# A two-layer graph attention kernel: full-width transpositions, one key product per half of the nodes, second-layer sums kept in PSUM

## The chip, the cores and the metric

One core of a Trainium2 chip runs the whole program. The metric is the device time of one execution in microseconds (us); a kernel's time is the median over its runs. The engines are named PE or TensorE (matrix products; PEld is its loading of weights), DVE or VectorE, ACT or ScalarE, POOL or GpSimd, and SP or SyncE, which only issues DMAs.

## What is computed

Eight graphs of 2048 nodes with 64 features share one 0/1 adjacency matrix (`adj`, 2048 x 2048 int32, denser for low node numbers). Two attention layers without learned scores are followed by two normalisations:

```python
def _gat_layer(h, mask, b):
    scores = jnp.einsum('...nd,...md->...nm', h, h)
    scores = jnp.where(mask, scores, -1e16)
    attn = jax.nn.softmax(scores, axis=-1)
    return jnp.einsum('...nm,...md->...nd', attn, h) + b

mask = graph + jnp.eye(N) > 0
h = jnp.einsum('bnc,hdc->bhnd', x, Wh)                  # 4 heads
cat = transpose(_gat_layer(h, mask, bh)).reshape(B, N, H * D)
z = leaky_relu(cat, 0.2)
h2 = jnp.einsum('bnk,dk->bnd', z, Wo)
z2 = leaky_relu(_gat_layer(h2, mask, bo), 0.2)
out = layernorm(z2) * gamma + beta
return layernorm(x + out)
```

## The kernel before

`gat_kernel` runs `fast_kernel` and then tests a flag; only where the flag is set does `general_kernel` run as well. In all runs told of here the flag stays 0. Everything below is `fast_kernel`, whose instructions stand in a hand-written order; each engine works through its own in that order.

The first 56 nodes ("hubs") attend to all nodes. The other 1992 are cut into 166 sets of 12 (nodes s, s + 166, ...), and a set attends only to the union of its members' neighbours, at most 128 nodes. So a set needs: a list of 128 node numbers (`index`), a gather of those nodes' rows for all eight graphs (`gather`, L727, an indirect DMA on POOL), the rows turned so that features lie on partitions (`turn`, L509), scores (L760 in the first layer, L923 in the second), a mask subtracted on DVE (L763, L928), an exp on ACT (L767, L931), and the weighted sum (values; L778, L943). A column of ones beside the features gives the softmax's denominator. All products are fp32; each of them appears in the trace as two matmul instructions.

The stages:

- *Hub stage*, `for i in range(NB)`, 16 blocks of 128 nodes. Per block: load x (L464, ACT's queue), save it as rows of `table1` in DRAM (L467, SP's queue), turn it (L509, tile `px`), two hub scores (L579), mask (L583), exp (L586), two hub values (L597). Beside this the adjacency is loaded in 48 pieces (`load_adj`, L647), turned into bf16 0/1 on POOL (L649), and summed with powers of two over a set's 12 members (`make_keys`, L669, on PE, in two rounds of 84 and 82 sets) into keys that hold a member mask and the node's number. `pick` then takes the 128 largest keys with max and match-replace on DVE (L684, L686); its jobs are spread over the loop by `some` and the hub stage's own loop. At most six blocks run before the first round is loaded, and three loads of the second round are issued per block from i = 8 on.
- `hub_end`, once per half of the graphs: the hubs' second-layer rows.
- *First-layer loop*, 83 groups of two sets, software-pipelined over i = -3 .. 85: gathers for group i + 5, scores i + 1, turn i + 3, `turn_values` (L789), `columns` (L743, the queries), values i + 1, `project` (L524, the head weights), `second_maps` (L800), `second_rows` (L805). PSUM has two tags with two buffers each, "s" (turn, scores) and "o" (oty, o, cat). `keep_rows` (L809) writes second-layer rows to `table2` in DRAM.
- *Second-layer hub*, w = -2 .. 8, on blocks of `table2`.
- *Second-layer units*, 42 units of four sets: `scores2`, `turn_group`, `values2`, whose sums are copied to SBUF (L947), written to DRAM (`back`, L950) and read back in blocks of ten sets (120 partitions) by `norm`, with 17 such norms as lists of jobs spread over later units. `norm` computes on DVE, with a square on ACT (L992) and a power on POOL (L998).
- The tail: the last norms, stores (L1035), the flag.

Of the kernel before, what the change touches and what calls it, by code (L numbers as in the profile page):

```python
# [27 lines left out]
F32 = mybir.dt.float32  # L29
# [328 lines left out]
def fast_kernel(ctx: ExitStack, tc: tile.TileContext, x, adj, Wh, bh, Wo, bo, gamma, beta, out, flag):  # L358
# [10 lines left out]
    ROW = B * K1  # L369
    NS = (N - HUB) // SET  # L370
    NG = NS // 2
    ROUNDS = ((0, 84), (84, NS - 84))
    M = SET * H
    HN = HUB // 2
    SEG, KEEP = 8, 32
    SW = N // SEG
    assert NS * SET == N - HUB and NG * 2 == NS

    const = ctx.enter_context(tc.tile_pool(name="const", bufs=1))
    rowp = ctx.enter_context(tc.tile_pool(name="rowp", bufs=12))  # L380
    work = ctx.enter_context(tc.tile_pool(name="work", bufs=2))
    small = ctx.enter_context(tc.tile_pool(name="small", bufs=4))
    psum = ctx.enter_context(tc.tile_pool(name="psum", bufs=2, space=bass.MemoryType.PSUM))
    dram = ctx.enter_context(tc.tile_pool(name="scratch", bufs=1, space=bass.MemoryType.DRAM))
    early_ctx = ExitStack()
    early = early_ctx.enter_context(tc.tile_pool(name="early", bufs=1))

    def two(name, tag="s"):

        return psum.tile([P, 2, 512], F32, tag=tag, name=name)  # L390
# [4 lines left out]
    def rows_tile(name):  # L395
        return rowp.tile([P, B, K1], F32, tag="rows", name=name)
# [6 lines left out]
    offdiag = const.tile([P, P], BF16, name="offdiag")  # L403
    nc.vector.tensor_scalar(offdiag, ident, -1.0, 1.0, OP.mult, OP.add)
    ones = const.tile([P, 1], F32, name="ones")
    nc.gpsimd.memset(ones, 1.0)
    shifts = const.tile([P, 3], F32, name="shifts")
    nc.gpsimd.memset(shifts[:, 0:1], -SHIFT1)
    nc.gpsimd.memset(shifts[:, 1:2], -SHIFT2)
    nc.gpsimd.memset(shifts[:, 2:3], EPS)  # L410
    mhalf = const.tile([P, B], F32, name="mhalf")
    nc.gpsimd.memset(mhalf, -0.5)
    bits = const.tile([P, SET], I32, name="bits")
    for k in range(SET):
        nc.vector.memset(bits[:, k:k + 1], N << k)
    powers = early.tile([84, SET, 84], BF16, name="powers")
    for k in range(SET):
        nc.vector.tensor_scalar(powers[:, k, :], ident[:84, :84], float(1 << k), None, OP.mult)
    number = early.tile([84, SEG, SW], U16, name="number")
    nc.gpsimd.iota(number, [[1, SEG], [SEG, SW]], base=0, channel_multiplier=0)  # L420

    wnat = early.tile([P, H, C], F32, name="wnat")
    whT = const.tile([P, H * D], F32, name="whT")
    gram = const.tile([P, H, P], F32, name="gram")
    wos = early.tile([D, H * D], F32, name="wos")
    woT = const.tile([P, HP, D], F32, name="woT")
    bhp = const.tile([P, HP], F32, name="bhp")
    bob = const.tile([P, D], F32, name="bob")
# [5 lines left out]
    back = dram.tile([NS, SET, ROW], F32, name="back")  # L434
    backh = dram.tile([HUB, 2, Q * K1], F32, name="backh")

    rall = const.tile([P, NG + 2, 8], F32, name="rall")
    NL = (NS + 9) // 10
    rall2 = const.tile([P, NL + 1, 8], F32, name="rall2")
    nc.gpsimd.memset(rall[:, NG:, :], 1.0)  # L440
    nc.gpsimd.memset(rall2, 1.0)
    over = const.tile([P, 2, SEG + 1], F32, name="over")
    nc.gpsimd.memset(over, 0.0)

    xT = const.tile([P, Q, N], F32, name="xT")
    own = const.tile([P, NG * 96 + 16], F32, name="own")
    nc.gpsimd.memset(own, 0.0)
    ownh = const.tile([P, 2, 2 * 2 * HN], F32, name="ownh")
# [4 lines left out]
    es = [const.tile([P, 912], F32, name=f"e{k}") for k in range(2)]  # L453
    rowts = [const.tile([P, 2, K1], F32, name=f"rowt{k}") for k in range(4)]
    for t in rowts:
        nc.gpsimd.memset(t, 1.0)
# [4 lines left out]
    def load_x(i):  # L461
        t = xrow[i] = rows_tile(f"x{i}")
        nc.vector.memset(t[:, :, D:K1], 1.0)
        nc.scalar.dma_start(out=t[:, :, :D], in_=x[:, i * P:(i + 1) * P, :].rearrange("b p c -> p b c"))  # L464

    def save_x(i):
        nc.sync.dma_start(out=table1[i * P:(i + 1) * P, :], in_=xrow[i].rearrange("p b k -> p (b k)"))  # L467

    hubraw = [early.tile([HUB, 2, 512], I32, tag="raw", name=f"hubraw{k}", bufs=3) for k in range(2)]
    load_x(0)  # L470
    for k in range(2):
        nc.sync.dma_start(out=hubraw[k], in_=adj[0:HUB, k * 1024:(k + 1) * 1024].rearrange("n (a m) -> n a m", a=2))
# [6 lines left out]
    nc.gpsimd.dma_start(out=bob, in_=bo.partition_broadcast(P))  # L479
    nc.gpsimd.dma_start(out=gam, in_=gamma.partition_broadcast(P))  # L480
    nc.gpsimd.dma_start(out=bet, in_=beta.partition_broadcast(P))
    load_x(2)
# [10 lines left out]
    nc.gpsimd.memset(gram, 0.0)  # L493
# [18 lines left out]
    def invert(op, r, osb, parts, k):  # L512

        v = op[:parts, :, :k * K1].rearrange("p s (q c) -> p s q c", q=k)
        nc.vector.reciprocal(r, v[:, :, :, D])
# [694 lines left out]
```

## Time and profile before

| | us |
|---|---|
| median of 3 runs (1602.45 to 1607.83) | 1607.18 |
| the profiled execution | 1601.0 |
| its span, first to last instruction | 1599.1 |
| PE busy | 1165.8 (73%), 35983 matmul instructions |
| DVE, ACT, POOL busy | 694.8, 439.3, 454.7 |
[...]

Durations of the sections below come from this one execution. Matmuls overlap: one row's duration is that from its start to its modelled end, so the pace of a group of matmuls is read from the start of a group to the start of the next. "issue" as a releaser means that the engine stood idle and the profile shows nothing that it waited for.

### The profile page before, as it was taken

Reading aid. Unit: us, or ns where it says so; the run is one execution under the profiler, and the core shown is the slowest. Engines: PE = TensorE matmul, PEld = TensorE weight load, DVE = VectorE, ACT = ScalarE, POOL = GpSimd, SP = SyncE. Lnnn points to the kernel's source line nnn. Section 1 sums busy time; section 2 is a strip of 40 time slices with the busy share of each in tenths; the row PEclk is TensorE's granted clock in tenths of the full one; section 3 lists DMA queues with packets and bytes.
Section 4 is the critical chain, followed back from the end, with each engine's and each line's share of the span. In section 5 each row is a group of like instructions: output and inputs, shape, how many; then the busy total and the mean of one; then the engine's idle time right before and its main releaser. Section 6 shows DMA issues by size and latency. Waiting matters only on the chain.

```text
span 1599.1 us, 76844 instructions
## 1 busy us (share of the span) xinstructions
PE 1165.8 (73%) x35983; PEld 1032.3 (65%) x35983; DVE 694.8 (43%) x1342; ACT 439.3 (27%) x735; POOL 454.7 (28%) x468
## 2 busy tenths in 40 slices
PE   5887643878788888888888876777777877777720
PEld 4565432777677777777777765676767766777620
DVE  5392210566554444444444441232444444445465
ACT  1111210333333333333433442221212212222210
POOL 6411113122222222222222200133434444343411
PEclk9756865999899999999999986777666677666755
DMA  7622113122222222222222203234454444444420
GB/s 168 180 78 72 68 62 99 46 76 77 62 79 82 73 76 81 77 72 75 78 77 75 77 13 129 69 97 119 109 139 110 109 119 135 114 118 115 126 65 18
DMA packets 98838, 144.45 MB, mean 90 GB/s; under 512 B 44608, under 2 KB 60944, under 8 KB 98512
## 3 DMA queue, kind: packets, MB, share of 16 engines
q0 software_dynamic: 26688, 88.51, 20.2%
q1 hardware_dynamic: 55184, 46.75, 10.3%
q10 hardware_dynamic: 16640, 4.20, 1.4%
q8 instruction: 284, 4.65, 1.2%
q14 instruction: 42, 0.34, 0.1%
HBM read 122.44 MB, written 16.97 MB: 87 GB/s over the span
## 4 chain that ended last, share of the span: by engine, by line
PE 53%; DMA 13%; issue 13%; DVE 11%; ACT 4%; POOL 2%; SPq 1%; another core or an unknown queue 1%; ACTq 0%; POOLq 0%; DVEq 0%
PE t L509 13%; DMA raw<-in_adj_dram 13%; PE s L923 12%; PE oty L743 6%; PE s L760 5%; DVE y L749 4%; PE o L943 3%; PE cat L524 3%; ACT otb L793 2%; PE oty L789 2%; PE cat L805 2%; PE cat L800 2%; POOL a L649 1%; DVE e L763 1%
## 5 line engine op out<-in xcount | busy, mean ns | idle before, releaser
L727 POOL DMA_INDIRECT g<-table,index x332 | 321.2, 967 | 872.0 <-PE o L778 464.1
L923 PE MATMUL s<-own,xTg 64*64 64x12 f32 x5312 | 197.6, 242 | 104.3 <-issue 102.9
L509 PE MATMUL t<-ident,g 64*64 64x64 f32 x10624 | 260.1, 262 | 16.0 <-issue 15.8
L923 PEld LDWEIGHTS s<-own,xTg 64*64 64x64 f32 x5312 | 171.0, 191 | 133.1 <-issue 127.3
L509 PEld LDWEIGHTS t<-ident,g 64*64 64x64 f32 x10624 | 243.1, 175 | 20.9 <-issue 20.2
L760 PE MATMUL s<-y,xTg 64*64 64x48 f32 x5312 | 121.7, 220 | 31.3 <-issue 31.1
L760 PEld LDWEIGHTS s<-y,xTg 64*64 64x64 f32 x5312 | 107.8, 134 | 41.7 <-issue 41.1
L743 PE MATMUL oty<-xT,gram 128*64 128x96 f32 x1280 | 125.0, 345 | 6.7 <-issue 6.7
L809 DVE COPY rowt<-cat 128x128 f32<-128x128 f32 x83 | 24.3, 293 | 213.4 <-ACT own L903 213.0
L749 DVE COPY y<-oty 128x384 f32<-128x384 f32 x80 | 68.8, 860 | 108.4 <-PE oty L743 108.4
L767 ACT ACTIVATE e<-e,shifts 128x768 f32<-128x768 f32 x83 | 77.7, 936 | 123.2 <-DVE e L763 123.2
L778 PEld LDWEIGHTS o<-g,e 128*64 128x64 f32 x2656 | 98.8, 144 | 11.5 <-ACT e L767 7.7
L778 PE MATMUL o<-g,e 128*64 128x65 f32 x2656 | 100.1, 228 | 7.4 <-ACT e L767 5.5
L743 PEld LDWEIGHTS oty<-xT,gram 128*64 128x64 f32 x1280 | 92.3, 149 | 17.2 <-issue 10.4
L649 POOL TENSOR_SCALAR a<-raw 84x1024 bf16<-84x1024 int32 (+1 forms) x48 | 49.8, 1037 | 183.2 <-DMA raw<-in_adj_dram 170.3
L531 ACT ACTIVATE z<-cat,bhp 128x192 f32<-128x192 f32 x166 | 60.8, 418 | 113.1 <-PE cat L524 109.8
L793 ACT COPY otb<-oty 128x384 f32<-128x384 f32 x83 | 39.7, 479 | 168.1 <-DVE y L749 152.5
L890 ACT COPY xTg<-t 128x1024 f32<-128x1024 f32 x83 | 84.5, 1018 | 4.6 <-PE t L509 4.6
L597 PEld LDWEIGHTS oh<-x,e 128*112 128x112 f32 x512 | 71.2, 229 | 19.8 <-ACT e L586 12.8
L597 PE MATMUL oh<-x,e 128*112 128x65 f32 x512 | 76.0, 317 | 10.6 <-ACT e L586 10.6
L998 POOL TENSOR_TENSOR st<-st,mhalf 120x8 f32<-120x8 f32 (+2 forms) x36 | 62.2, 1728 | 71.7 <-DVE st L997 42.4
L996 DVE TENSOR_REDUCE st<-sq 120x8 f32<-120x512 f32 (+2 forms) x36 | 24.7, 685 | 131.9 <-ACT sq L992 96.2
(151 smaller groups left out, 1544.4 us busy)
## 6 DMA issues: line engine op xcount, KB each, us to landing
raw<-in_adj_dram SPq DMA_DIRECT2D x24, 336.0 KB
raw<-in_adj_dram SPq DMA_DIRECT2D x24, 328.0 KB
g<-table,index POOLq DMA_INDIRECT x332
table<-x SPq DMA_DIRECT2D x16, 260.0 KB
gh<-table SPq DMA_DIRECT2D x16, 260.0 KB
x<-in_x_dram ACTq DMA_DIRECT2D x16, 256.0 KB
table<-rowt SPq DMA_DIRECT2D x166, 24.4 KB
back<-o2sb SPq DMA_DIRECT2D x164, 24.4 KB
```

What stands on the lines that cost most here:

```text
L509: nc.tensor.matmul(v[half(p), r, j, q, :], rows[half(r), 2 * q + p, :D], ident[half(r), half(r)], start=True, stop=True)
L597: nc.tensor.matmul(hubo[t][:HW // 2, s, b * K1:(b + 1) * K1], e[:, c0:c0 + HW // 2], xrow[i][:, 4 * t + b, :], start=(i == 0 and b == 0), ...
L649: nc.gpsimd.tensor_scalar(a[:n], raw[:n], 1.0, 0.0, OP.min, OP.max)
L727: nc.gpsimd.indirect_dma_start(out=t.rearrange("p b k -> p (b k)"), out_offset=None, in_=table, in_offset=bass.IndirectOffsetOnAxis(ap=ind ...
L743: nc.tensor.matmul(py[half(p), h // 2, 192 + h % 2 * 96:192 + (h % 2 + 1) * 96], gram[:, h, half(p)], src, start=True, stop=True)
L749: nc.vector.tensor_copy(y.rearrange("p n (a b) -> p a b n", a=2), py[:, :, 192:384].rearrange("p a (b n) -> p a b n", b=2))
L760: nc.tensor.matmul(sp[half(r), p, (q * 2 + j) * M:(q * 2 + j + 1) * M], xt[half(p), r, j, q, :], y[half(p), (j * Q + q) * M:(j * Q + q + 1 ...
L767: nc.scalar.activation(e[:, :16 * M], e[:, :16 * M], AF.Exp, bias=shifts[:, 0:1], scale=1.0)
L778: nc.tensor.matmul(op[half(p), j, q * K1:(q + 1) * K1], e[:, c0:c0 + 64], rw[:, 2 * q + p, :], start=True, stop=True)
L793: nc.scalar.copy(ot.rearrange("c h (p n) -> c h p n", p=2), pt[:, :, :Q * M].rearrange("c p (n h) -> c h p n", h=H))
L890: nc.scalar.copy(t, tp)
L923: nc.tensor.matmul(sp[half(r), p, c0:c0 + SET], xt[half(p), r, s % 2, q, :], own[half(p), (s * Q + q) * SET:(s * Q + q + 1) * SET], start= ...
```

## The change

`turn` uses `nc.tensor.transpose` with a 128 x 128 identity: rows of two graphs lie side by side (`[P, Q, PW]`, PW = 130, a one at both ends), and one instruction turns both. `columns` uses the whole block-diagonal `gram`, on contiguous copies made on POOL (`own_rows`). The adjacency is loaded with members and sets together on 120 partitions, so one product over all members gives a key. `second_rows` and `turn_values` also become transposes. The first-layer loop gets a new order and four PSUM tags with one buffer each (S, T, C, O); `keep_columns` moves from DVE to ACT, the copy to `own` from ACT to DVE, and `keep_values` becomes two copies. Nine of 34 adjacency pieces and the second `pick` move into this loop. In the second layer row tiles have 20 buffers, all turned rows are copied on ACT, `values2` sums two units into one PSUM tile (the second adds to the columns that zeros in its weights leave alone), and `norm` reads them there; x for it is loaded from `x`, and `bo` is added in `keep_rows`. There are 21 norms of two units, and one for the hubs. The core of the diff:

```diff
-    def turn(tp, j, rows):
-        v = tp.rearrange("c r (j q i) -> c r j q i", j=2, q=Q)
+    def turn(tp, rows):
         for q in range(Q):
-            for p in range(2):
-                for r in range(2):
-                    nc.tensor.matmul(v[half(p), r, j, q, :], rows[half(r), 2 * q + p, :D], ident[half(r), half(r)],
-                                     start=True, stop=True)
+            nc.tensor.transpose(tp[:, q * P:(q + 1) * P], rows[:, q, 1:1 + P], ident)
...
     def hub_values(i, t):
+        for v in range(2):
             for k in range(2):
                 for p in range(2):
-                    nc.tensor.matmul(hubo[t][:HW // 2, s, b * K1:(b + 1) * K1], e[:, c0:c0 + HW // 2],
-                                     xrow[i][:, 4 * t + b, :], ...)
+                    for u in range(2):
+                        nc.tensor.matmul(hubo[t][half(u), v, ...], es[t][:, c0:c0 + 64],
+                                         xrow[i][:, 2 * t + k, sums(p)], ...)
...
     def load_adj(r, t, m):
-        raw = early.tile([84, 2, 512], I32, tag="raw", name=f"raw{r}_{c}_{t}", bufs=3)
-        nc.sync.dma_start(out=raw[:n], in_=byset[s0:s0 + n, 2 * t:2 * t + 2, c * 512:(c + 1) * 512])
+        raw = early.tile([120, NCH], I32, tag="raw", name=f"raw{r}_{t}_{m}", bufs=3)
+        nc.sync.dma_start(out=raw[:np_], in_=byset[:, s0:s0 + ns, m * NCH:(m + 1) * NCH])
...
+    def own_rows(g):
+        t = held["x", g] = work.tile([P, GM], F32, tag="xo", name=f"xo{g}", bufs=3)
+        src = xT[:, :, HUB:].rearrange("c q (k s) -> c s q k", s=NS)[:, 2 * g:2 * g + 2]
+        nc.gpsimd.tensor_copy(t.rearrange("c (s q k) -> c s q k", s=2, q=Q), src)
...
     for i in range(-3, NG + 3):
...
+        sp = one(f"s{i}", "S")
+        if 0 <= i - 3 < NG:
+            second_rows(i - 3, sp[:GM, 1, 384:512])
+        if 0 <= i - 2 < NG:
+            second_maps(i - 2, sp[:, 0, 384:384 + GM])
         if 0 <= i + 1 < NG:
+            scores(i + 1, sp)
+            weigh(i + 1, sp)
+        if 0 <= i < NG:
+            turn_values(i, op)
+            keep_values(i, op)
+        if 0 <= i + 3 < NG:
+            tp = one(f"t{i + 3}", "T")
+            for j in range(2):
+                turn(tp[:, j, :], rows[1, 2 * (i + 3) + j])
+        if i < NG:
+            cat = one(f"cat{i}", "C")
+        if 0 <= i + 3 < NG:
+            columns(i + 3, cat)
+        if 0 <= i < NG:
+            project(held.pop(("ot", i)), cat, GM)
+        if 0 <= i + 1 < NG:
+            op = one(f"o{i + 1}", "O")
+            values(i + 1, op)
...    # then DVE: own, keep_rows, leak, some(2), invert, some(3); ACT: xTg, leaky, keep_columns
     def values2(op, sets, e, a, more):
         for k, s in enumerate(sets):
             rw = rows.pop((2, s))
             for f in range(2):
                 for t in range(4):
+                    q, p = 2 * f + t % 2, t // 2
+                    nc.tensor.matmul(op[t * 32:(t + 1) * 32, f, k * W2 + p:k * W2 + p + K1], e[:, p * Q + q, k, :],
+                                     rw[:, q, sums(p)], start=(a == 0 and k == 0), stop=(k >= more), ...)
-        nc.scalar.copy(o[:, :nb], op[:, :nb, :4 * K1])
-        for t in range(4):
-            nc.sync.dma_start(out=dst, in_=...)          # to back
...
+    for u in range(-1, NU + 6):
+        if u + 4 < NU:
+            for s in sets[u + 4]:
+                gather(table2, s, 2, rows2)
+        a = (u + 1) % 2
+        if u + 1 < NU:
+            scores2(bank2(f"s2_{u + 1}", "S"), sets[u + 1], es2[a], a)
+        if u + 3 < NU:
+            turn2(u + 3)
+        if u + 1 < NU:
+            if a == 0:
+                op = bank2(f"o2_{u + 1}", "O")
+            values2(op, sets[u + 1], es2[a], a, len(sets[u + 2]) if a == 0 else 0)
+            if a == 1:
+                spread(u, norm_sets((u + 1) // 2, op))
+        work_on(u)
```

## Rows read from the trace of the kernel before

**Rows 1.** Busy time by stage: PE, PEld, DVE, ACT, POOL (instructions), clock, DMA share, GB/s.

```profile
0.00:80.00 80.00, 57.39 (x631) 42.45 (x631) 38.95 (x84) 14.34 (x18) 42.20 (x61) 0.87 0.71 174
80.00:258.00 178.00, 108.59 (x1104) 83.43 (x1103) 62.97 (x151) 28.49 (x33) 30.20 (x40) 0.65 0.20 67
258.00:284.00 26.00, 11.70 (x113) 8.77 (x115) 4.03 (x10) 3.14 (x8) 10.42 (x11) 0.50 0.45 126
284.00:959.00 675.00, 552.41 (x19587) 502.24 (x19584) 319.57 (x643) 264.96 (x498) 145.68 (x154) 0.98 0.26 71
959.00:1019.00 60.00, 37.61 (x1295) 33.57 (x1298) 10.43 (x20) 15.82 (x16) 9.40 (x10) 0.73 0.36 113
1019.00:1532.00 513.00, 397.69 (x13280) 361.76 (x13275) 223.69 (x366) 108.35 (x155) 204.74 (x186) 0.69 0.42 113
1532.00:1599.00 67.00, 0.36 (x10) 0.09 (x2) 35.20 (x72) 4.19 (x8) 12.07 (x7) 0.50 0.16 40
```

**Rows 2.** Longest waits between 80 and 258 us: us in total, times, longest.

```profile
POOL a L649 <- DMA raw<-in_adj_dram: 144.3, 22, 17.0
```

**Rows 3.** PE in order of time, hub blocks: start us, us, count.

```profile
220.32 0.99 PE L579 MATMUL sh<-yh,xT 64*64 64x224 f32 x16
221.24 1.79 PE L597 MATMUL oh<-x,e 128*112 128x65 f32 x16
...
51.02 3.25 PE L597 MATMUL oh<-x,e 128*112 128x65 f32 x16
```

**Rows 4.** PE in order of time, one first-layer group; idle time and releaser in brackets.

```profile
738.92 1.52 PE L743 MATMUL oty<-xT,gram 128*64 128x96 f32 x16
740.26 1.12 PE L778 MATMUL o<-g,e 128*64 128x65 f32 x32
741.98 0.44 PE L805 MATMUL cat<-ident,own 128*64 128x128 f32 x4 [0.61 <-ACT otb L793]
...
744.04 0.87 PE L760 MATMUL s<-y,xTg 64*64 64x48 f32 x43 [0.41 <-issue]
...
744.77 1.13 PE L509 MATMUL t<-ident,g 64*64 64x64 f32 x62
```

**Rows 5.** PE in the last first-layer groups, and the window table around them.

```profile
945.57 1.10 PE L760 MATMUL s<-y,xTg 64*64 64x48 f32 x64
946.49 0.65 PE L789 MATMUL oty<-ident,osb 48*64 48x48 f32 x32
949.00 1.25 PE L778 MATMUL o<-g,e 128*64 128x65 f32 x32 [1.87 <-ACT e L767]
...
933.50:949.50 16.00, 11.68 (x516) 10.96 (x510) 7.53 (x14) 7.52 (x16) 0.00 (x0) 1.00 0.05 13
```

**Rows 6.** Groups by line and form: busy us, mean ns, idle before and releasers.

```profile
L793 ACT COPY otb<-oty 128x384 f32<-128x384 f32 x83 | 39.7, 479 | 168.1 <-DVE y L749 152.5 <-DVE rall L515 15.7
...
L684 DVE MAX8 cand<-keys 82x8 f32<-82x256 f32 x32 | 13.1, 417 | 0.3
...
L700 PE MATMUL pb<-ident,best 84*128 84x84 f32 x1 | 0.4, 372 | 2.2 <-DVE best L684 2.2
```

**Rows 7.** Second-layer units: a turn on PE, two window rows, the groups' line for scores2.

```profile
1300.27 3.71 PE L509 MATMUL t<-ident,g 64*64 64x64 f32 x125
...
1305.60:1310.60 5.00, 2.96 (x57) 2.40 (x57) 0.16 (x1) 1.12 (x2) 3.14 (x4) 0.77 0.57 160
1311.00:1316.00 5.00, 5.00 (x208) 4.93 (x211) 2.00 (x5) 0.62 (x2) 1.67 (x1) 0.59 0.34 85
...
L923 PE MATMUL s<-own,xTg 64*64 64x12 f32 x5312 | 197.6, 242 | 104.3 <-issue 102.9 <-DVE xTg L1148 0.4
```

**Rows 8.** PE in order of time, in hub_end.

```profile
272.54 1.02 PE L618 MATMUL hh<-zh,woT 128*64 128x112 f32 x8 [8.40 <-issue]
```

**Rows 9.** The tail: DVE and SP's queue in order of time.

```profile
1538.93 0.20 DVE L973 RECIPROCAL rall<-y 120x8 f32<-120x8 f32 x1 [5.97 <-DMA y<-back]
...
1560.74 29.80 SPq L1035 DMA_DIRECT2D out_dram<-y  x24
```

More of the change, by code (lines that the diff above doesn't have):

```diff
@@ L723, in fast_kernel, with gather @@
     held = {}
-    def gather(table, s, layer):
-        t = rows[layer, s] = rows_tile(f"g{layer}_{s}")
-        nc.gpsimd.indirect_dma_start(out=t.rearrange("p b k -> p (b k)"), out_offset=None, in_=table,
+    def gather(table, s, layer, new):
+        t = rows[layer, s] = new(f"g{layer}_{s}")
+        nc.gpsimd.indirect_dma_start(out=t.rearrange("n q c -> n (q c)"), out_offset=None, in_=table,
                                      in_offset=bass.IndirectOffsetOnAxis(ap=index[:, s:s + 1], axis=0))
-    def turn_group(layer, g, tag):
-        tp = two(f"t{layer}_{g}", tag)
-        for j in range(2):
-            turn(tp, j, rows[layer, 2 * g + j])
-        t = work.tile([P, 2, 512], F32, tag="xTg", name=f"xTg{layer}_{g}", bufs=3)
-        held["T", layer, g] = t
-        return tp, t
@@ L818, in fast_kernel, with some @@
     hub_columns()
+    picks = []
+    def some(n):
+        for _ in range(n):
+            if picks:
+                picks.pop(0)()
+    for e in es:
+        nc.vector.memset(e[:, 4 * HW:], 1.0)
     pend = None
-    pieces = list(load_adj_jobs)
-    picks = []
     for i in range(NB):
@@ L874, in fast_kernel @@
         if 0 <= i - 1 < NG:
             leak(held["z", i - 1])
+        if 0 <= i + 3 < NG:
+            t = held["T", 1, i + 3] = work.tile([P, 2, 512], F32, tag="xTg", name=f"xTg{i + 3}", bufs=3)
+            nc.scalar.copy(t, tp)
+        if 0 <= i < NG:
+            held["z", i] = leaky(cat, GM, f"z{i}")
+        if 0 <= i + 3 < NG:
+            keep_columns(i + 3, cat)
         if i >= 0:
             some(2)
[L878 to L881 removed]
@@ L882, in fast_kernel @@
-        if 0 <= i < NG:
-            turn_values(i, oty)
-        if 0 <= i + 3 < NG:
-            columns(i + 3, oty)
-            keep_columns(i + 3, oty)
-        if 0 <= i < NG:
-            keep_values(i, oty)
-        if 0 <= i + 3 < NG:
-            nc.scalar.copy(t, tp)
         if 0 <= i + 1 < NG:
-            values(i + 1)
+            invert(i + 1, op)
         if i >= 0:
-            cat = two(f"cat{i}", "o")
-        if 0 <= i - 2 < NG:
-            second_rows(i - 2, cat[:, 1, 256:384])
@@ L897, in fast_kernel @@
-        if 0 <= i - 1 < NG:
-            second_maps(i - 1, cat[:, 0, 256:384])
-        if 0 <= i < NG:
-            project(held.pop(("ot", i)), cat, 96)
-            held["z", i] = leaky(cat, i, 96)
-        if 0 <= i - 1 < NG:
-            nc.scalar.copy(own[:, (i - 1) * 96:i * 96], cat[:, 0, 256:352])
-        if 0 <= i - 2 < NG:
-            keep_rows(i - 2, cat[:, 1, 256:384])
-        if i >= 0:
-            some(1)
-    assert not picks
-    early_ctx.close()
-    late = ctx.enter_context(tc.tile_pool(name="late", bufs=2))
@@ L915, in scores2 @@
-    def scores2(sp, sets, e):
-        n = len(sets) * SET
+            more(2)
+            some(3)
+            done = all(t // 3 > k3 for r, t, m in pieces)
+            if k3 < nk and done:
+                make_keys(1, k3, late_two)
+                k3 += 1
+                if k3 == nk:
+                    picks = pick(1)
+    assert not picks and not pieces and k3 == nk
+    begin.close()
+    stage.close()
+    late = ctx.enter_context(tc.tile_pool(name="late", bufs=2))
+    psum2 = ctx.enter_context(tc.tile_pool(name="psum2", bufs=1, space=bass.MemoryType.PSUM))
@@ L1110, in fast_kernel @@
             hub_turn(w + 1)
+        elif w + 1 < NB // 2 + 2 and w + 1 >= NB // 2:
+            turn2(w + 1 - NB // 2)
         if 0 <= w - 1 < NB // 2:
             hub_values2(w - 1)
-    o = late.tile([P, 2, 4 * K1], F32, tag="o2", name="o2h")
-    nc.scalar.copy(o[:, 0], oh2[:, 0, :Q * K1])
-    for p in range(2):
-        nc.sync.dma_start(out=backh[:, p, :], in_=o[p * 64:p * 64 + HUB, 0, :])
-    NU = (NS + 3) // 4
-    sets = [list(range(4 * u, min(4 * u + 4, NS))) for u in range(NU)]
-    jobs = {}
```

740 lines of the change are left out of this document (394 added, 346 removed).

## The prediction

> **What bounds the kernel now.** I read the stage table first [rows 1], because an average over the program hides five different limits. Its rows show the hub stage up to 258 us, hub_end, the first-layer loop (675 us for 83 groups, 8.1 us each with filling and draining), the second-layer hub (60 us), the second-layer units (513 us for 42, 12.2 us each) and a tail of 67 us. They add up to the span of 1599.1 us; the profiled execution reports 1601.0 us, and the median of the runs is 1607.18 us, so I put 2 us and then 6 us on top of a sum of stages.
>
> In the hub stage the adjacency loads set the pace after 80 us. Traffic falls from 174 to 67 GB/s there while the DMA engines are only 20% busy [rows 1], and the conversions of the 24 loads with 82 partitions wait 144.3 us for data [rows 2]. A load that keeps few engines busy is slow; it is not that bandwidth is used up. PE itself needs, where nothing holds it, 0.99 us for hub scores and 1.79 us for hub values, and 3.25 us for the values when its clock is at half [rows 3].
>
> In the first-layer loop PE is the bound: its groups follow each other [rows 4], with 0.61 us of waiting for ScalarE and some tenths in which the profile names no releaser. The clock is 0.98 [rows 1].
>
> In the second-layer units PE runs at a mixed clock of 0.69 [rows 1] and is also starved of instructions. In 5.0 us beside four gathers on GpSimd it starts 57 matmuls, in 5.0 us without them 208 [rows 7]; the matmuls of scores2 alone stand 102.9 us behind "issue" [rows 7]. The same hits others: in hub_end PE loses 8.40 us this way [rows 8], while GpSimd issues gathers (11 instructions in that stage [rows 1]). In the tail VectorE waits 5.97 us for rows written to DRAM and read back, and the last 24 stores are queued on SP for 29.80 us [rows 9].
>
> **The change, part by part.**
>
> *Hub stage.* The loads become 120 partitions of 4 KB (12 members by 10 sets, half a row). No row shows this shape. If it runs as the first 24 loads did, at 174 GB/s [rows 1], 25 loads of 0.49 MB, 4.2 MB of x and 4.3 MB of saved rows are 20.8 MB, or 120 us, below what the engines need. Per block i, PE does two hub scores, two hub values (now 16 half-width products instead of 8) and one transposition. Half-width values take 1.12 us for 32 instructions [rows 4], so a block takes 2 x (0.99 + 1.12) + 4 x 0.14 = 4.8 us at full clock, and 1.8 times that, 8.7 us, at half (3.25 / 1.79 [rows 3]). I take 7.7 us: the clock is 0.65 there [rows 1], and for some seven blocks VectorE has six pick jobs each beside its other work (some 0.9 us a job: 0.42 [rows 6], about the same again for replacing and a little for loading). Sixteen blocks are 123 us (80 to 160). With 26 us of hub_end [rows 1], which the early gathers starve as before, and about 25 us of beginning, the loop starts at 175 us instead of 284 (150 to 210): **-109 us**. The memsets and selections that move on GpSimd's queue stand ahead of its conversions, a few us that the hub mask on VectorE hides; without that cover they delay the first block by as much.
>
> *The price of a transposition.* Each is now one instruction of 128 columns over the whole array, in place of four products of 64 columns that are two instructions each. Nearest rows: the values, 35 ns for 65 columns on half the array (1.12 us / 32 [rows 4]), thus 70 ns for both halves and 138 ns for 128 columns. Below it stands one old turn instruction, 18 ns (1.13 us / 62 [rows 4]); above it the kernel's only true transpose, 372 ns, alone and not pipelined [rows 6]. I take 0.14 us at full and 0.28 us at half clock.
> [...]
>
> *First-layer loop.* Removed per group: 56 of 64 turn instructions, 28 of 32 in turn_values, 3 of 4 in second_rows, 8 of 16 in columns, whose strided read moves to GpSimd as own_rows. Twelve transpositions are 1.7 us against 1.13 + 0.65 us [rows 4, 5], a draw; columns falls from 1.34 us (738.92 to 740.26) to about 0.7. But order and PSUM change too: one buffer per tag, and project now stands ahead of values, behind keep_values, which waits on ScalarE behind the exp. So I count the chain, not PE. The last groups, which have neither turn nor columns, show it bare: scores from 945.57, values at 949.00 after 1.87 us of waiting [rows 5]; less 1.0 us of scores this is 2.4 us for subtracting and exp. Added: keep_values, now two copies, 0.7 us (between one of 0.48 us [rows 6] and two of them). Then project 0.4, values 1.12, second_maps 0.45, second_rows 0.1 and scores 1.0 us. The sum is 2.4 + 0.7 + 0.4 + 1.1 + 0.5 + 1.0 = 6.1 us. PE's 1.7 + 0.7 us of other work lie in the 3.1 us before project, so they cost nothing; at half clock they would be 4.8 us and stick out. Two gathers a group still starve scores (0.4 us here: 744.04 stands 0.41 us late [rows 4]), so 6.6 us (6.1 to 7.6). keep_columns moves to ScalarE, behind leaky: whose turn it delays is the next exp, 2 us away. own and keep_rows on VectorE stand behind weigh, ahead of invert; GpSimd's own_rows stands behind two gathers that had idled. Bias rows (bob) in keep_rows cost nothing there.
> 83 x 6.6 = 548 us. The second pick runs inside the loop: 58 jobs at five a group are 4.5 us on VectorE beside some 3.2 (319.57 us [rows 1] less some 50 of picks, over 83), so about twelve groups take 7.9 us, +16. Filling and draining, one group longer, 21. Together 585 us for 675: **-90 us** (-130 to 0).
>
> *Second-layer hub.* Scores of both blocks now go before either subtraction, but exp, the copy of xTg and scores still follow each other. 57 us for 60: **-3** (-12 to +5).
>
> *Second-layer units.* Scores2 (128 instructions) and values2 (64) stay; 128 turn instructions, 3.8 us at 30 ns [rows 7], become 16 transpositions, 2.2 to 4.5 us. All 320 take 7.7 us at the rate of the better window; the other 4.5 of 12.2 us are starvation and hand-overs. GpSimd's gathers, with 20 row buffers, no longer wait for values2, but stand behind the power operations of the norms in GpSimd's queue, which come once a unit; so the burst drifts toward scores2 again. I take 11.0 us (9 to 12.4): -0.3 for turn, -0.9 for 96 matmuls that can no longer be starved. VectorE loses the copy of xTg and gains nothing. Values2 of a pair's first unit waits for the previous pair's first norm step; 1.5 us, under scores2. SP's per-pair 16 issues replace about as many. 42 x 11.0 + 3 = 465 us: **-48 us** (-135 to +8).
>
> *Tail.* Sums are read from PSUM, so the trip to DRAM goes, and one pair's norm with the rest of three others remains: some 20 us of VectorE, 5 us of hand-overs, 10 us for eight stores (29.80 / 24 each [rows 9]), 1 us for the flag. 36 us for 67: **-31 us** (-40 to -15).
>
> **Sum.** 175 + 585 + 57 + 465 + 36 = 1318 us of span, 1320 us as the profiled execution tells it, and 1325 us beside the median.
>
> **The rivals.**
> *(A) The units gain nothing*: half clock makes 16 transpositions 4.5 us and the burst meets scores2 in full, 12.4 us a unit, +59: 1384 us. For it: the 0.69 clock; against: fewer instructions to starve.
> *(B) The first-layer loop falls to half clock.* [...] Against: in the last groups the clock stayed at 1.00 for 16 us with 1.87 us of waiting a group [rows 5]. Then the chain's PE part, 3.0 us, becomes 5.4 and the period 8.5: 83 x 1.9 = +158, 1483 us.
> [...]
> *(C) The new load shape is as slow as the old second round*: hub stage unchanged, nine more loads in the loop, +110: 1435 us.
> *(D) Starvation goes with the instructions*: 8.7 us a unit, -97: 1228 us.
> *(E) Slower.* Single buffers put everything on one chain. If PE runs at half clock and each of its two bursts costs the chain 1.1 us (two gathers are half of the 5.0 us in which 151 of 208 starts are lost [rows 7]), a group takes 8.5 + 2.2 = 10.7 us, +340: 1665 us. It decides from 10.0 us a group ((675 + 191 - 37) / 83), where it has eaten the 191 us gained elsewhere. Against it: starvation hides in PE's waiting.
>
> **How the numbers follow.** Forecast 0.45, A 0.22, D 0.15, B 0.08, C 0.05, E 0.05. The range, 1225 to 1455 us, takes in the forecast's own bounds (1240 to 1420), A, C and most of D; B, E and the rest of D are left out, under two in ten. A measurement of this kernel can tell about 0.3%. Only E is slower: faster 0.94, same 0.01, slower 0.05.
>
> **What would show it.** Hub: the loop's first turn near 175 us and DMA above 100 GB/s before it. Loop: 6 to 7 us between values, PE waiting for ScalarE ahead of project, clock near 1. Units: 16 instead of 128 turn matmuls each, gaps in scores2 beside gathers. Tail: no wait for DRAM. I am wrong if the loop's clock falls, if project waits for more than exp and keep_values, or if a transposition costs over 0.2 us at full clock.

## The result and the profile after

The changed kernel takes 1391.67 us (median of four runs, 1388.97 to 1392.80) beside 1605.24 us for the kernel before in the same runs: a ratio of 0.867, 95% interval 0.8645 to 0.8689. That is 214 us faster, within the range of 1225 to 1455 us, and 67 us above the forecast of 1325. Its profiled execution has a span of 1390.4 us.

The stages of the changed kernel, in the columns of [rows 1]: from, to, length, then PE, PEld, DVE, ACT and POOL busy (instructions), clock, DMA share, GB/s. In order: hub stage, hub_end, first-layer loop, second-layer hub, units, tail.

```profile
0.00:152.00 152.00, 102.95 (x1717) 72.05 (x1717) 83.69 (x184) 42.85 (x51) 59.74 (x136) 0.94 0.60 157
152.00:166.40 14.40, 6.32 (x58) 3.90 (x58) 4.28 (x13) 2.64 (x6) 0.00 (x0) 0.65 0.02 5
166.40:829.00 662.60, 541.88 (x11724) 465.03 (x11724) 287.93 (x735) 291.47 (x581) 192.91 (x257) 0.98 0.29 78
829.00:887.00 58.00, 38.57 (x876) 32.43 (x876) 11.39 (x21) 19.38 (x20) 18.78 (x22) 0.80 0.53 166
887.00:1360.00 473.00, 358.48 (x8600) 321.52 (x8596) 205.59 (x389) 127.76 (x163) 219.56 (x187) 0.71 0.38 101
1360.00:1390.40 30.40, 0.19 (x2) 0.11 (x2) 18.93 (x41) 1.89 (x3) 8.52 (x5) 0.50 0.13 28
```

Against the terms of the sum:

| stage | before | forecast | after | forecast missed by |
|---|---|---|---|---|
| start of the loop | 284 | 175 | 166.4 | -8.6 |
| first-layer loop | 675 | 585 | 662.6 | **+77.6** |
| second-layer hub | 60 | 57 | 58 | +1 |
| units | 513 | 465 | 473 | +8 |
| tail | 67 | 36 | 30.4 | -5.6 |

One term is wrong, and by more than the whole miss: the loop got 12 us shorter where 90 were forecast. So the question is what holds a group at 7.74 us (the distance from one exp to the next in the steady part) when its chain was counted at 6.1.

Here is one group of it, PE and then POOL in order of time (start us, us, line, operands, count; in brackets the idle time before and its releaser):

```profile
571.11 0.84 PE L792 MATMUL s<-y,xTg 64*64 64x48 f32 x32
572.35 0.34 PE L792 MATMUL s<-y,xTg 64*64 64x48 f32 x6 [0.41 <-issue]
573.11 0.66 PE L792 MATMUL s<-y,xTg 64*64 64x48 f32 x26 [0.41 <-issue]
573.70 0.60 PE L831 MATMUL o<-ident,osb 112*128 112x112 f32 x4
574.14 1.04 PE L510 MATMUL t<-ident,g 128*128 128x128 f32 x8
575.01 1.03 PE L778 MATMUL cat<-xo,gram 128*128 128x96 f32 x8
576.55 0.56 PE L529 MATMUL cat<-otb,whT 64*64 64x96 f32 x16 [0.51 <-ACT otb L839]
577.04 1.15 PE L814 MATMUL o<-g,e 128*64 128x65 f32 x32
...
570.27 0.97 POOL L765 DMA_INDIRECT g<-table,index  x1 [1.49 <-PE o L814]
571.55 0.95 POOL L765 DMA_INDIRECT g<-table,index  x1 [0.30 <-issue]
```

And one of the last groups, for which nothing is left to gather:

```profile
800.39 1.15 PE L792 MATMUL s<-y,xTg 64*64 64x48 f32 x64
801.47 0.60 PE L831 MATMUL o<-ident,osb 112*128 112x112 f32 x4
801.90 1.04 PE L510 MATMUL t<-ident,g 128*128 128x128 f32 x8
802.78 1.03 PE L778 MATMUL cat<-xo,gram 128*128 128x96 f32 x8
804.34 0.56 PE L529 MATMUL cat<-otb,whT 64*64 64x96 f32 x16 [0.53 <-ACT otb L839]
804.83 1.15 PE L814 MATMUL o<-g,e 128*64 128x65 f32 x32
```

Without gathers the 64 matmuls of scores go from 800.39 to 801.47, 1.08 us; with them from 571.11 to 573.70, 2.59 us, with two gaps that stand behind "issue". Everything else in the two groups is alike, even the 0.5 us that PE waits for ScalarE ahead of project, and the groups without gathers follow each other in 6.25 us. The 1.5 us of difference is the whole gap between 6.25 and 7.74, and it falls at the same place in each group, because the gathers are released by the last product of values ("PE o L814") and scores comes soon after.

### The profile page after: what moved, and what is told of

Its sections match the earlier page's. It is cut to its first block, busy times and chain, and to the rows that moved or that the text cites. A ratio compares the mean times of both kernels' runs of the same rounds, so it can differ in the third digit from the quotient of the medians.

```text
span 1390.4 us, 50953 instructions
## 1 busy us (share of the span) xinstructions
PE 1048.4 (75%) x22965; PEld 895.0 (64%) x22965; DVE 611.8 (44%) x1380; ACT 486.0 (35%) x823; POOL 499.5 (36%) x606
## 4 chain that ended last, share of the span: by engine, by line
PE 52%; issue 21%; DVE 14%; ACT 7%; POOL 3%; DMA 2%; ACTq 1%; SPq 0%; POOLq 0%; DVEq 0%
PE s L1031 12%; PE t L510 10%; PE s L792 9%; PE o L814 6%; DVE e L797 5%; ACT otb L839 4%; PE o L1049 4%; PE cat L529 3%; PE s L848 3%; PE s L851 1%; POOL a L643 1%; PE s2h L1178 1%; DVE cand L708 1%; DVE e L575 1%; PE sh L571 1%
## 5 line engine op out<-in xcount | busy, mean ns | idle before, releaser
L510 PE MATMUL t<-ident,g 128*128 128x128 f32 x1328 | 228.6, 336 | 2.8 <-issue 1.8
L510 PEld LDWEIGHTS t<-ident,g 128*128 128x128 f32 x1328 | 201.1, 177 | 6.3 <-issue 3.7
L1089 POOL TENSOR_TENSOR st_s<-st_s,mhalf 128x8 f32<-128x8 f32 x42 | 76.8, 1829 | 209.4 <-DVE st_s L1088 209.4
L797 DVE TENSOR_TENSOR e<-s,mask 128x768 f32<-128x768 f32 x82 | 78.5, 957 | 137.3 <-PE s L792 137.2
L821 DVE RECIPROCAL rall<-o 64x8 f32<-64x8 f32 x166 | 34.0, 205 | 208.4 <-PE o L814 207.3
L1219 ACT COPY xTg<-t 128x1024 f32<-128x1024 f32 x83 | 83.4, 1012 | 40.5 <-PE t L510 40.2
L814 PE MATMUL o<-g,e 128*64 128x65 f32 x2656 | 97.3, 227 | 0.0
L814 PEld LDWEIGHTS o<-g,e 128*64 128x64 f32 x2656 | 85.7, 139 | 10.0 <-issue 0.2
L981 ACT COPY xTg<-t 128x1024 f32<-128x1024 f32 x83 | 87.3, 1052 | 5.4 <-PE t L510 5.4
L529 PE MATMUL cat<-otb,whT 64*64 64x96 f32 x1328 | 46.9, 257 | 47.5 <-ACT otb L839 47.5
L778 PE MATMUL cat<-xo,gram 128*128 128x96 f32 x640 | 82.5, 272 | 0.0
L778 PEld LDWEIGHTS cat<-xo,gram 128*128 128x128 f32 x640 | 78.0, 192 | 0.0
L529 PEld LDWEIGHTS cat<-otb,whT 64*64 64x64 f32 x1328 | 31.1, 133 | 61.1 <-ACT otb L839 60.9
```

The lines of the kernel that those rows point to most:

```text
L510: nc.tensor.transpose(tp[:, q * P:(q + 1) * P], rows[:, q, 1:1 + P], ident)
L529: nc.tensor.matmul(cat[half(j), s, hp * n:(hp + 1) * n], whT[half(s), h * D:(h + 1) * D], ot[half(s), h, :], start=True, stop=True)
L778: nc.tensor.matmul(cat[:, h // 2, (2 + h % 2) * GM:(3 + h % 2) * GM], gram[:, h, :], xo, start=True, stop=True)
L797: nc.vector.tensor_tensor(e[:, :16 * M].rearrange("p (a q n) -> p a q n", a=2, q=Q), sp[:, :, :8 * M].rearrange("p a (q n) -> p a q n", q= ...
L814: nc.tensor.matmul(op[half(p), j, o0:o0 + K1], e[:, c0:c0 + 64], rw[:, q, sums(p)], start=True, stop=True)
L981: nc.scalar.copy(t, tp)
```

## The experiments

The theory: gathers on GpSimd keep PE from its instructions for some 0.75 us each (half of the 1.5 us of a group), and what that costs depends on what PE has to do just then. The main rival: the chain is longer than counted for another reason, and the gaps fall into time that PE would wait anyway.

**No gathers.** In `gather`:

```
+        if s >= 12:
+            rows[layer, s] = held["first", layer, s % 12]
+            return
...
```

> The changed kernel without its row gathers after the first 12 of each layer: later groups and units reuse the first 12 row tiles (so the gathering is left out, and the masks are set to zero, so that no sum vanishes). Theory: TensorE's matmuls of scores stand behind 'issue' because of the gathers, 1.5 us a group, and nothing else lengthens the chain. Then the first-layer loop turns in 6.25 us, as in its last groups, instead of 7.74, and lasts about 545 us instead of 663; scores take 1.1 us instead of 2.6; the second-layer units take 8 to 9 us instead of 11.3; the span falls to about 1160 us. Rival: my chain was too short by 1.5 us for another reason (single PSUM buffers, a ScalarE queue that is too full), and the gaps beside the gathers only fill time in which TensorE would wait anyway; then the period stays at 7.5 to 7.7 us and ScalarE or VectorE ends the wait.

With sums over other nodes the flag sends this kernel and the next two through the general path afterwards (7420 us and more in all, one run each); only their stages are read. Rows of the steady loop and of the units:

```profile
340.00:741.00 401.00, 361.16 (x8815) 318.51 (x8814) 182.87 (x448) 219.01 (x441) 20.15 (x58) 0.99 0.05 11
790.00:1076.00 286.00, 241.64 (x8760) 223.23 (x8760) 211.46 (x402) 128.98 (x168) 73.39 (x41) 0.89 0.13 30
```

PE in order of time, in one of its units:

```profile
957.05 1.11 PE L1052 MATMUL o<-g,es 128*32 128x65 f32 x64
958.09 2.38 PE L1034 MATMUL s<-own,xTg 64*64 64x12 f32 x128
```

The period is 6.25 us from the end of the second pick on, as expected. The units fall from 11.35 to 6.49 us, further than the 8 to 9 expected: scores2 takes 2.38 us, and the clock in the units rises from 0.71 to 0.89. The rival, a longer chain, is out.

**Plain loads from SyncE, and from GpSimd.** What is it about a gather, the rows' traffic or the issuing?

```
-        nc.gpsimd.indirect_dma_start(out=..., in_=table, in_offset=bass.IndirectOffsetOnAxis(ap=index[:, s:s + 1], axis=0))
+        nc.sync.dma_start(out=..., in_=table[s % NB * P:(s % NB + 1) * P, :])      # second kernel: nc.gpsimd
```

> The changed kernel with each gather of 128 scattered rows replaced by a plain load of 128 neighbouring rows of the same table and size, issued by SyncE (the gathering is left out, and the masks are set to zero). The same bytes go into the same tiles, but GpSimd issues nothing. If GpSimd's issuing is what keeps instructions from TensorE: period 6.25 us, scores 1.1 us, units 8 to 9 us, span about 1160 us. If it is the rows' traffic on the DMA engines: period 7.5 to 7.7 us, units about 11 us, span about 1390 us.

> As the run with plain loads from SyncE, but the plain loads are issued by GpSimd (the gathering is left out, and the masks are set to zero). If any DMA whose list GpSimd makes costs TensorE its instructions: about 7.7 us a group, as with gathers. If only the indirect form does: 6.25 us a group. If the traffic of the rows is the cause, both runs with plain loads show 7.5 to 7.7 us.

Behind the second pick both loops turn in 6.25 us, and a unit takes 7.42 us (SyncE) and 7.16 us (GpSimd). In the run with plain loads from GpSimd, POOL and then PE in one group:

```profile
505.00 1.07 POOL L765 DMA_DIRECT2D g<-table  x2 [1.55 <-PE o L813]
...
505.79 1.15 PE L791 MATMUL s<-y,xTg 64*64 64x48 f32 x64
```

The two loads start at the same place, ahead of scores, and move as many bytes (93 GB/s over this loop, 78 in the changed kernel's), yet scores is whole. So neither the amount of traffic nor the fact that GpSimd issues is the cause; only the indirect form is. By what way it reaches PE's instructions, no run here shows, nor whether it is the index or the scattered rows: none gathers neighbouring rows through an index.

**The loop's gathers later.** Nothing is left out here, only moved:

```
+            if i >= 0:
+                nc.gpsimd.tensor_copy(stamp, held["o", i][:1, 0, 0, :1])
             for j in range(2):
                 gather(table1, 2 * (i + LOOK) + j, 1, rows_tile)
```

> The changed kernel, everything computed; in the first-layer loop GpSimd copies one element of the previous group's osb ahead of each pair of gathers, so that the pair starts when invert ends, some 1.3 us later than now, and its stalls fall on turn_values, turn and columns instead of scores. There TensorE has 20 long instructions (2.2 us) and 0.5 us of waiting ahead of project. Theory with stalls that hit any instruction, 1.5 us a group: 2.2 + 1.5 - 2.7 = 1.0 us sticks out, the period is about 7.2 us and the time falls by some 45 us. Theory with stalls that only hit a dense row of short matmuls (64 scores in 1.1 us): 6.3 us a group, and the time falls by 110 to 120 us. Rival (the chain is longer for another reason): no change.

It takes 1316.55 us, a ratio of 0.817 (0.8115 to 0.8231), 75 us less than the changed kernel. One group:

```profile
508.08 0.97 POOL L766 DMA_INDIRECT g<-table,index  x1 [0.55 <-PE s L793]
509.36 1.07 POOL L766 DMA_INDIRECT g<-table,index  x1 [0.30 <-PE t L511]
...
506.61 1.15 PE L793 MATMUL s<-y,xTg 64*64 64x48 f32 x64
507.69 0.60 PE L832 MATMUL o<-ident,osb 112*128 112x112 f32 x4
508.12 1.04 PE L511 MATMUL t<-ident,g 128*128 128x128 f32 x8
509.00 1.03 PE L779 MATMUL cat<-xo,gram 128*128 128x96 f32 x8
```

The same two gathers now run beside 16 long instructions, which are not delayed by a hundredth. Project and values behind them, whose instructions start every 31 and 34 ns, keep their time too (0.49 and 1.08 us), and the period is 6.25 us, as without gathers. So in this loop the stall costs only a dense row of short matmuls (64 in 1.08 us), the second of the two theories. The gain was 75 us and not 110 to 120: some 60 groups gain 1.48 us each, but the first 18 lose 14 us together, since VectorE still picks there (five jobs a group), invert ends late and the gathers wait for it, so that several groups take about 10 us instead of some 8.

**Both bursts later.** That is mended, and the units' four gathers are put behind the subtraction of scores2:

```
-            if i >= 0:
+            if k3 == nk and not picks:
...
             scores2(bank2(f"s2_{u + 1}", "S"), sets[u + 1], es2[a], a)
+        if u + 4 < NU:
+            nc.vector.memset(marks[a], 0.0)
+            nc.gpsimd.tensor_copy(stamp, marks[a])
+            for s in sets[u + 4]:
+                gather(table2, s, 2, rows2)
```

> As the run that starts the loop's gathers later (everything computed), with two differences: the loop's gathers are held back only once the second pick is done, since VectorE sets the pace before that; and in the second-layer units the four gathers start behind the subtraction of scores2 instead of ahead of it, so that they run beside turn2 (16 long instructions) and values2. The loop: 6.25 us a group after the picks, first groups as in the changed kernel, so some 20 us less than in the run before. Units: theory of starvation that hits dense rows of short matmuls: turn2 hides the first two gathers, values2 (64 instructions) and the start of the next scores2 take the rest; 8.5 to 9.5 us a unit instead of 11.3, -75 to -120 us; the time is 1180 to 1225 us. Rival: GpSimd's four gathers and power operation (7.2 us) and the stalls fill the unit wherever they stand; then the units stay at 11 us and the time is 1290 to 1300 us.

1272.76 us, ratio 0.794 (0.7894 to 0.7976): faster than the run before it, but a unit went to 10.39 us only, where 8.5 to 9.5 were expected, and so the time missed the 1180 to 1225 us expected. One unit of the changed kernel, and then one of this one:

```profile
1153.35 0.40 PE L1031 MATMUL s<-own,xTg 64*64 64x12 f32 x10
...
1157.64 2.96 PE L1031 MATMUL s<-own,xTg 64*64 64x12 f32 x100 [1.08 <-issue]
1160.53 3.20 PE L510 MATMUL t<-ident,g 128*128 128x128 f32 x16
1163.66 1.11 PE L1049 MATMUL o<-g,es 128*32 128x65 f32 x64
```

```profile
1009.06 2.69 PE L1034 MATMUL s<-own,xTg 64*64 64x12 f32 x128
1011.68 3.67 PE L511 MATMUL t<-ident,g 128*128 128x128 f32 x16
1015.28 1.52 PE L1052 MATMUL o<-g,es 128*32 128x65 f32 x44
1017.62 0.28 PE L1052 MATMUL o<-g,es 128*32 128x65 f32 x3 [0.82 <-issue]
1019.04 0.47 PE L1052 MATMUL o<-g,es 128*32 128x65 f32 x17 [1.15 <-issue]
```

Scores2 falls from 7.2 us to 2.6, but values2 rises from 1.1 to 4.2: the four gathers run from 1013.25 to 1018.05, so they start 1.6 us into turn2, whose long instructions cover 2.0 us of the 4.8, and values2 takes the rest. My estimate let values2 off too cheaply. The clock stays at 0.71 in these units.

**The burst between the two.** The gathers are asked for one unit earlier and wait for the buffers that values2 leaves, once with two fills ahead of them, once without:

```
-        if u + 4 < NU:
-            for s in sets[u + 4]:
-                gather(table2, s, 2, rows2)
+        for v in ((3, 4) if u < 0 else (u + 5,)):
+            if v < NU:
+                for s in sets[v]:
+                    gather(table2, s, 2, rows2, 2 if s % 4 == 0 else 0)     # fills of the tile ahead; 0 in the second kernel
```

> As the run with both bursts moved (everything computed), but in the units the gathers are asked for one unit earlier, into the buffers that values2 has just left, with two fills of a row tile on GpSimd (1.0 us) ahead of them instead of the mark behind scores2. There the four gathers started 1.5 us into turn2 and values2 took 4.24 us instead of 1.1. Now they start some 1.6 us behind the end of values2, that is 1.1 us before scores2 ends, and their stalls (from 1.2 us after the start) cover turn2 (3.7 us) first. Theory: values2 falls to 2 to 3 us, the unit from 10.4 to 8.5 to 9.3 us, the time from 1273 to 1195 to 1230 us. Rival: what is left of the unit is GpSimd's own chain (four gathers, power operation, fills: 8 us) or the norms on VectorE; then nothing changes or it gets slower.

> As the run before it, without the two fills: the gathers start right behind values2, 1.0 us earlier, and their stalls begin in the second half of scores2 and end with turn2, so values2 is whole (1.1 to 1.9 us) and scores2 pays instead (4 us for 2.7). Theory: within 0.5 us a unit of the run with the fills (which of the two rows of short matmuls pays makes little difference), 1185 to 1250 us. If the place of the burst does not matter, both runs stay at 1273 us.

The first takes 1261.35 us (0.788, 0.7825 to 0.7942), not to be told from the run before it, where 1195 to 1230 were expected; the second 1311.07 us (0.822, 0.8189 to 0.8257), where 1185 to 1250 were expected. In the second the 128 matmuls of scores2 take the burst again (7.45 us, from 1007.65 to the start of turn2) and a unit takes 11.31 us. I had expected the two within 0.5 us a unit; their times are 50 us apart, 1.2 us for each of 42 units. Which short row pays does matter, and no place tried here hides four gathers: without indirect gathers the units are at 6.5 to 7.4 us.

**Turning by products again**, as before, in the changed kernel (readers of the turned rows take the old order):

```
-            nc.tensor.transpose(tp[:, q * P:(q + 1) * P], rows[:, q, 1:1 + P], ident)
+            for p in range(2):
+                for r in range(2):
+                    nc.tensor.matmul(v[half(p), r, j, q, :], rows[half(r), q, 1 + p * D:1 + (p + 1) * D], ident[half(r), half(r)], ...)
```

> The changed kernel with turn alone undone: 16 products of 64 rows for each row tile, as before, instead of 4 transpositions (consumers read the old order). If a transposition is a draw (0.11 us each against 1.13 us for 64 products): first-layer period 7.7 to 8.0 us (turn stands in the wait ahead of project, and the burst of the gathers still falls on scores), units 11.5 to 12.5 us since 128 products can be starved where 16 transpositions can not, hub stage up to 5 us more; the time rises by 10 to 80 us. If the transposition is what makes the change fast, the loop and the units both go back to before's 8 and 12.2 us: +60 us and more. If the time does not rise by 0.3%, transposing brings nothing by itself.

1440.78 us, ratio 0.898 (0.8937 to 0.9022): 49 us of the 214 go with turn's transpositions. In its stages (the changed kernel's in brackets) the units take 500 us (473), the second-layer hub 64 (58) and the loop 675 (663). The steady period of the loop is the same, 7.75 us (7.74); most of the loop's 12 us lie in its first four groups (37 us for 29), and why they are slower is not shown.

```profile
606.84 0.66 PE L797 MATMUL s<-y,xTg 64*64 64x48 f32 x26 [0.41 <-issue]
607.43 0.60 PE L836 MATMUL o<-ident,osb 112*128 112x112 f32 x4
607.96 1.16 PE L513 MATMUL t<-ident,g 64*64 64x64 f32 x64
609.05 1.13 PE L783 MATMUL cat<-xo,gram 128*128 128x96 f32 x8
```

32 products in 64 instructions take 1.09 us (607.96 to 609.05) where 8 transpositions take 0.87 (574.14 to 575.01): 0.109 us each. In the loop that lies in PE's wait ahead of project, and the same two gaps stand in scores. In the units it is not the turn itself that counts: it takes 3.64 us here (1156.70 to 1160.34; its row is 3.71 us long, as that of [rows 7], where the clock is 0.50) and 3.60 in the changed kernel (1172.00 to 1175.60, at 0.50). A unit is 0.6 us longer (11.95 for 11.35), spread over scores2, values2 and turn, at a clock of 0.68 for 0.71.

**The load shape alone, in the kernel before.**

```
-    ROUNDS = ((0, 84), (84, NS - 84))
+    ROUNDS = ((0, 84), (NS - 84, 84))
```

> The kernel before, with one line changed: the second round of the adjacency covers sets 82 to 165 (84 partitions) instead of 84 to 165 (82 partitions); two sets are done twice. Theory: a load with 82 partitions keeps few DMA engines busy, whatever its bytes; with 84 the second 24 loads run like the first (3 to 4 us instead of 7), traffic after 80 us stays above 130 GB/s, and the hub stage is bounded by TensorE at 160 to 190 us instead of 258: the time falls by 60 to 95 us. Rival: the loads of the second round are slow since the stores of x and the first round's stand in the same queue, or since GpSimd's conversions hold the buffers; then nothing changes (within 10 us).

1534.86 us, ratio 0.958 (0.9521 to 0.9635): 70 us. Its first three stages, columns as above; [rows 1] has 67 GB/s and a DMA share of 0.20 for the second:

```profile
0.00:80.00 80.00, 54.31 (x644) 40.24 (x648) 40.93 (x89) 14.34 (x18) 43.33 (x63) 0.91 0.78 185
80.00:190.00 110.00, 95.82 (x1106) 75.09 (x1106) 61.49 (x148) 28.69 (x33) 38.34 (x49) 0.79 0.46 128
190.00:206.00 16.00, 9.05 (x94) 6.24 (x96) 2.73 (x6) 3.14 (x8) 0.95 (x1) 0.50 0.08 20
```

The time is within the 60 to 95 us forecast, and traffic, at 128 GB/s, just below the 130. Two partitions more make the loads faster: GpSimd's conversions wait 22.2 us for them between 80 and 190 us, where they waited 144.3 [rows 2]. And hub_end loses the gathers beside it (16 us for 26). The loop starts 78 us earlier, so most of the 118 us that the change gains ahead of the loop can be had by this one line. The trace of before agrees with the theory of few busy engines: of the 2 KB packets, in which these loads move, 2.0 are under way at a time on average between 80 and 258 us (82 partitions) and 9.6 between 20 and 80 us (84 partitions), counted while any is. Why two partitions make that difference is not shown.

**Plain loads in the kernel before**, the edit as above, in its `gather`:

> The kernel before with each gather replaced by a plain load of 128 neighbouring rows issued by GpSimd (the gathering is left out, and the masks are set to zero; the flag is held at zero). It tells what the gathers cost before the change. If I under-priced them because the old loop hid them: TensorE's instructions follow each other there, so the loop falls from 8.0 to 7.2 to 7.6 us a group (the 0.4 us of rows 4), the units from 12.2 to 7.5 to 9 us; the time falls to 1360 to 1450 us. If the old loop lost as much as the new one: 6.5 us a group, and the time is below 1350 us.

It takes 1485.37 us in its one run, more than the 1360 to 1450 expected. Rows of its loop and its units:

```profile
274.00:925.00 651.00, 535.83 (x19585) 494.09 (x19581) 319.83 (x643) 264.56 (x498) 82.75 (x155) 0.95 0.25 74
980.00:1418.00 438.00, 328.94 (x13076) 305.68 (x13075) 222.72 (x367) 107.09 (x154) 131.99 (x184) 0.66 0.44 131
```

The old loop gains 24 us (0.29 us a group) and the old units 75 (1.8 us each), both less than expected. The fastest groups of the loop fall from 7.36 to 6.57 us, but other gaps behind "issue" remain, with or without gathers, such as

```profile
769.57 0.26 PE L788 MATMUL oty<-ident,osb 48*64 48x48 f32 x3
771.39 0.67 PE L788 MATMUL oty<-ident,osb 48*64 48x48 f32 x29 [1.55 <-issue]
```

Counted over the starts of PE's matmuls, the old loop has 30 gaps of 1.0 us and more between 340 and 940 us (41 us together), and 43 between 340 and 905 us with plain loads (71 us); the changed loop has one, where it drains, also when its gathers are moved. The traces show what most of these gaps stand behind. The profile has a DMA queue that it names "instruction"; in the old loop with plain loads (packets, MB, share of 16 engines):

```profile
q8 instruction: 136, 2.23, 1.6%
```

Its packets have 16 KB, and there is one for some 250 of PE's matmuls and weight loads (the changed kernel has 183 packets for 45930 of them). In 37 of the 43 gaps PE starts again 1.15 to 1.65 us behind the end of such a packet, where 12% of all moments lie. It is so in 46 of the 52 gaps of the old units with plain loads (103 us together, for 14 gaps and 19 us with gathers, so these units lose most of their gain again) and in 20 of the 21 in the units of the run without gathers, but in only 1 of the 26 in the changed kernel's units, beside gathers. So two different things stand behind "issue". The second looks like PE waiting for the next piece of its program; no run varies that alone.

## Why the prediction was right, and where it was not

**Hub stage: mechanism right, 9 us too dear.** The stage runs at 157 GB/s, and GpSimd waits 32.5 us for loads in it. The turns of the 16 blocks follow each other in 7.9 us on average (21.3 to 139.7 us), near the 7.7 forecast, but only one of the two reasons given holds: the clock was 0.94, not 0.65, while VectorE with the picks does set the pace for a good part (of the chain from 80 to 128 us, 28.7 of 48 us lie on it). The closest turns stand 4.4 to 4.6 us apart, near the 4.8 worked out for full clock. Hub_end takes 14.4 us where I kept 26, which is more than the whole miss: its gathers are over by then (POOL has no instruction there).

**Price of a transposition: a fifth too dear.** It took 0.109 us at a clock of 1.00 (8 from 574.14 to 575.01; 0.14 taken); in the units 16 take 3.60 us at 0.50 (1172.00 to 1175.60; with both bursts moved 3.60 us too, 1011.68 to 1015.28), 0.225 us each (0.28 taken). The four products of columns, 96 columns each and 8 instructions together, take 1.03 us where 8 transpositions of 128 columns, one instruction each, take 1.04 (575.01 and 574.14): by the column a transposition is 2.6 times as fast as a product in these two rows. Columns was put at 0.7 us and takes 1.03, off the path.

**First-layer loop: the mis-sized term.** The chain of 6.1 us was right (6.25), and its cover too: PE waits 0.51 us for ScalarE ahead of project. What failed is the step "Two gathers a group still starve scores", by its size: read there as 0.4 us, it was allowed 0.5, and it measured 1.5, over 83 groups 83 us more. With 0.15 us a group of chain (12 us), and 17 us less for filling, draining and the second pick (20 us beside 83 groups of 7.74, for 37), that is the miss of 78.

Two readings went wrong. First, I priced the stall by the one gap named "issue" in [rows 4]; beside each gap the matmuls start slowly as well (the two gaps are 0.82 us of the 1.5). Second, I let the old price stand for the new loop. In the group of [rows 4] the kernel before has

```profile
741.19 0.94 POOL L727 DMA_INDIRECT g<-table,index  x1 [6.49 <-PE o L778]
742.44 0.95 POOL L727 DMA_INDIRECT g<-table,index  x1 [0.30 <-issue]
...
743.06 0.56 PE L760 MATMUL s<-y,xTg 64*64 64x48 f32 x18
```

Values release the gathers there too, but project stands between values and scores, so the first gather starts 1.9 us ahead of scores and only the second has its stall in them. In the new order the first starts 0.84 us ahead (570.27 and 571.11), and both stalls fall on scores, which lie on the one chain that sets the period. That order was readable: the release of the gathers and the row that follows values stand in the two kernels. In the old loop the gathers cost 0.8 us in the best groups and 0.29 on average, since other gaps took their place.

A group with picks takes mostly 7.8 to 8.3 us, with and without gathers, near the 7.9 forecast; beside groups of 7.74 that is little, and only without the stall does it show. One group takes 16.8 us (212.8 to 229.6): GpSimd waits 14.5 us there for an adjacency piece of those moved into the loop, for which the sum had no term.

**Units: right (11.3 us for 11.0), and open to a correction.** The turn products went and the burst met scores2, as forecast. Rival D (starvation goes with the instructions) was far off, and for a reason: scores2 kept its 128 short matmuls. I called 4.5 of 12.2 us starvation and hand-overs in the old units; with plain loads the old units lose 1.8 us and the new ones 4.2 (11.35 to 7.16), since in the old ones the gaps behind instruction packets come in place of the gathers'.

**Tail:** 30.4 us for 36; VectorE has no wait for DRAM left, and its last chain is 1.0 and 1.75 us of waiting for GpSimd's power operation among 18.93 us of work.

**Rivals.** A's time (1384) is nearest to the result, by chance: it let the units gain nothing, and they gained 40 us. B did not happen: the clock is 0.98 in the loop with 13 of 141 matmuls transposing. C is refuted by the 157 GB/s. E put each burst at 1.1 us of the chain (by the rows that it cites, 3.6 us of lost starts beside four gathers, it is 0.9), nearer to the 0.75 measured than my 0.2 to 0.25; as the clock did not fall, it stayed far from its 10.0 us.

## What to carry over

A stall that the trace shows beside an engine's short instructions has to be priced by the time that the row takes with and without it, not by the idle time in brackets, and it has to be priced anew for the place where the change puts it. Where an indirect gather can't be avoided, let its release put it beside long instructions: one copied element ahead of the loop's gathers was worth as much here as a third of the whole rewrite (75 of 214 us). Before counting instructions as cost or gain, look whether they are on the path: 56 fewer a group did nothing for this loop's steady period. And where a row shows "issue", ask which kind of gap it is before taking away a cause: in the old kernel taking the gathers away mostly made room for the other kind.

## What the runs showed of the hardware

- In these loops an indirect gather on GpSimd (0.95 to 1.07 us) cost PE 0.75 us in a row of matmuls that start every 17 ns, and nothing in rows that start every 31 to 110 ns. A plain load of the same bytes, from GpSimd or SyncE, cost nothing in the first row either (6.25 us a group).
- The clock records in the traces of before and of the changed kernel hold two levels, 1.00 and 0.50. In the changed kernel's units the granted clock falls behind a burst of gathers: in the unit at 1153.35 it is 0.84 over the 4.3 us in which PE starts 31 matmuls, then 0.50 in the 2.9 us of dense scores2, 0.59 in turn2 and 1.00 in values2. Over all its units it is 0.71 with gathers, also where values2 has the gaps, and 0.82 to 0.89 without; in the kernel before it is 0.69 with gathers and 0.66 with plain loads. Turn2 takes 3.60 us at 0.50 (1172.00 to 1175.60) and 1.90 at 1.00 (955.15 to 957.05 in the run without gathers), so in these units the rows behind such a burst pay for it again.
- Where PE starts some 30 matmuls a microsecond (29.2 in the old loop, 30.4 with plain loads, 28.8 in the new units with plain loads), gaps of 1.0 us and more appear that no gather explains, most of them right behind a 16 KB instruction packet; at 18.5 to 25.5 the loop has one, where it drains.
- The fastest kernels here, with both bursts moved, take 1261 and 1273 us. What holds a unit at 10.4 us in the second of them is known in part only: values2 takes the rest of the burst (4.1 us of a unit on average, 1.4 without gathers), and the clock stays low.
